# Scan's main loop written in a fixed order, with six groups' output products as seven block products in place of eight

## The chip, the cores and the metric

The kernel runs on one core of one Trainium2 chip. It is one launch for one layer of a network: a graph cross-attention, then a state-space scan, then a feed-forward part. The metric is the device time of the core in microseconds (us), lower is better. A core has a matrix engine (PE, whose weight loads are listed apart as PEld), a vector engine (DVE), a scalar engine (ACT), a general engine (POOL) and a queue that issues transfers (SP). Each engine runs its own instructions in the order in which they were put in its queue, and waits at an instruction until what that instruction needs is there. SBUF is the on-chip memory; PSUM is the small memory that PE writes its results to; the scan uses eight banks of it, each a tile of 128 partitions by 512 fp32 numbers.

## The reference, cut to what matters

Only the scan part (`_L0_attn_ref`) is touched. Its input is 16 sequences of 32 tokens, 512 tokens in all, 512 numbers each, all fp32. In outline:

```python
h = x * rsqrt(mean(x * x) + EPS) * norm_w
proj = einsum('bsd,od->bso', h, in_proj_w)         # gate 8192, hidden 8192, B and C 1024 each, dt 128
hBC = silu(causal_conv(hBC, conv_w, conv_b))       # 4 taps along the sequence
dt = softplus(dt + dt_bias);  A = -exp(A_log)      # 128 heads
L = exp(segsum(A * dt))                            # decay between two tokens of a sequence, per head
M = einsum('bcihn,bcjhn->bcijh', C, B) * L         # C and B are shared by the 16 heads of a group
y = einsum('bcijh,bcjhp->bcihp', M, hid * dt) + Dp * hid
yg = y * silu(gate)
ygr = yg * rsqrt(mean over the group's 1024 (yg * yg) + EPS)     # 8 groups
out = residual + einsum('bsd,od->bso', ygr * gnorm_w, out_proj_w)
```

The 8192 inner channels are 64 tiles of 128 channels; a group is 8 tiles (16 heads). So the scan is 8 groups of 8 tiles, and the output product sums over all 64 tiles.

## The kernel before, in words

The graph part comes first and takes the first 1300 us or so; the scan follows, and the feed-forward part ends the kernel. The scan first makes what all groups share: `hT` (the normed input, transposed: channels on partitions, tokens along the row), `dt` and `dA`, and `CB`, the products of C and B for each group (lines 1166 to 1247).

Then the main loop (lines 1347 to 1352) goes over the 8 groups. Its three stages:

- `inner(g)` makes the gate `gs` and the hidden values `hid` of a group. For each of its 8 tiles there are two projections (`project`, line 1181: four fp32 products of 128x128 weights with 512 tokens, accumulated in a PSUM bank of the pool `ps_p`, two banks). The gate gets a Silu on ACT (line 1260). The hidden tile gets its convolution (`convolve`): ACT writes the first tap out of PSUM (line 1188), DVE adds the three others, also out of PSUM (line 1193, three instructions), and ACT applies Silu (line 1196). With every tile from the second group on, one step of `parts` is taken: it loads small low-rank weights for the feed-forward part (nine small transfers for each piece) and splits a piece that came earlier into three bf16 parts, eight DVE instructions of 18 partitions (lines 167 to 173). There are ten pieces.
- `mix(g)` is the scan itself, tile by tile. PE transposes the hidden tile (`pht`, line 1289), DVE scales it by `dt` into `hd` (line 1291). For every second tile `decays` makes the decays of four heads: POOL multiplies `lei` by `dA` into `da` (line 1269), PE sums it (`pl`, line 1274), ACT takes the exponential `ed` (line 1279). DVE multiplies `ed` by `CB` into two tiles `el` (line 1302), PE makes the eight small products `py` (line 1310), DVE adds the skip term into `hid` (line 1314) and multiplies by the gate into `gs` (line 1315). ACT squares `gs`, POOL adds the squares into `ssq` (line 1321), ACT scales `gs` by `gnorm_w` (line 1322).
- `close(g)` makes the group's share of the output. PE sums `ssq` over the channels (`pn`, line 1329), DVE and ACT make the inverse root from it (line 1331 and the helper `rstd`, lines 70 to 80). The eight tiles `wo` of the output weights are loaded (line 1337). For each of the four blocks of 128 tokens, PE adds up eight products of 128x128 by 512 columns in a bank of `ps_o` (line 1342), and DVE adds the result, times the inverse root, into the residual `xt` (line 1345).

In the source `inner(g + 1)` stands ahead of `mix(g)` and `close(g)`, but the source does not set the order: a scheduler reorders the instructions of the whole kernel on every engine by its own priorities, within what data and buffers allow. Each tile comes from a pool, and a tag with `bufs` of n has n slots; a new tile waits until the one n before it on that tag has been read for the last time. The pools that count here: `ps_p`, `ps_m` (for `pht` and `pl`), `ps_y` (for `py` and `pn`) and `ps_o`, two PSUM banks each; six slots for the projection weights `win`; ten for `wo`; three for `hd` and `el`, two for `da`.

An fp32 product is two instructions on PE, so a profile counts two for each product in the source.

Of the kernel before, what the change touches and what calls it, by code (L numbers as in the profile page):

```python
# [8 lines left out]
F32 = mybir.dt.float32  # L9
# [3 lines left out]
AF = mybir.ActivationFunctionType  # L13
ALU = mybir.AluOpType
# [4 lines left out]
P = 128  # L19
B = 16  # L20
C = 32
D = 512
# [9 lines left out]
CB = 3  # L32
# [1083 lines left out]
def scan_part(nc, tc, cx, I, id32, ones, xt, u, rstd, lows):  # L1116
# [58 lines left out]
    def project(t, tag):  # L1175

        w = wpool.tile([P, 4, P], F32, tag="win", name=f"win{tag}", bufs=6)
        nc.sync.dma_start(out=w, in_=I["in_proj"][t])
        pp = ps_p.tile([P, D], F32, tag="p", name=f"pp{tag}")
        for k in range(4):  # L1180
            nc.tensor.matmul(pp, lhsT=w[:, k], rhs=hT[:, k], start=(k == 0), stop=(k == 3))  # L1181
        return pp

    def convolve(dst, t, tag):

        pp = project(NT + t, f"c{tag}")
        y = wk.tile([P, B, SEQ], F32, tag="cy", name=f"cy{tag}", bufs=3)
        nc.scalar.activation(  # L1188
            y.rearrange("p b s -> p (b s)"), pp, AF.Identity, bias=cb[:, t:t + 1], scale=cw[:, t, 3:4]
        )  # L1190
        pv = pp.rearrange("p (b s) -> p b s", b=B)
        for sh in (1, 2, 3):
            nc.vector.scalar_tensor_tensor(  # L1193
                y[:, :, sh:], pv[:, :, :SEQ - sh], cw[:, t, 3 - sh:4 - sh], y[:, :, sh:], ALU.mult, ALU.add
            )
        nc.scalar.activation(dst, y.rearrange("p b s -> p (b s)"), AF.Silu)


    wdt = wpool.tile([P, 4, P], F32, tag="win", name="wdt", bufs=6)
# [50 lines left out]
    parts = lows.load(low)  # L1250
    big = cx.enter_context(tc.tile_pool(name="sbig", bufs=2))

    def inner(g):

        gs = big.tile([P, TG, D], F32, tag="gs", name=f"gs{g}")
        hid = big.tile([P, TG, D], F32, tag="hid", name=f"hid{g}")
        for i in range(TG):
            t = g * TG + i
            pg = project(t, f"g{t}")
            nc.scalar.activation(gs[:, i], pg, AF.Silu)  # L1260
            convolve(hid[:, i], t, f"h{t}")
            if g > 0:
                next(parts, None)
        return gs, hid

    def decays(h):

        da = sm.tile([P, 4, 4, SEQ], F32, tag="da", name=f"da{h}", bufs=2)
        nc.gpsimd.tensor_tensor(  # L1269
            da, lei.unsqueeze(1).unsqueeze(1).to_broadcast([P, 4, 4, SEQ]),  # L1270
            dA[:, :, h:h + 4].rearrange("p q h -> p h q").unsqueeze(3).to_broadcast([P, 4, 4, SEQ]), ALU.mult,
        )
        pl = ps_m.tile([P, 4, 4, SEQ], F32, tag="m", name=f"pl{h}")
        nc.tensor.matmul(  # L1274
            pl.rearrange("p h q i -> p (h q i)"), lhsT=gt, rhs=da.rearrange("p h q i -> p (h q i)"),
            start=True, stop=True,
        )
        ed = sm.tile([P, 4, 4, SEQ], F32, tag="ed", name=f"ed{h}", bufs=2)
        nc.scalar.activation(ed, pl, AF.Exp)
        return ed  # L1280

    def mix(g, gs, hid):

        ssq = wk.tile([P, D], F32, tag="ssq", name=f"ssq{g}")
        for i in range(TG):
            t = g * TG + i
            pt = ps_m.tile([P, 4, P], F32, tag="m", name=f"pht{t}")
            for q in range(4):
                nc.tensor.transpose(pt[:, q], hid[:, i, q * P:(q + 1) * P], id32)
            hd = sm.tile([P, 4, 2, 64], F32, tag="hd", name=f"hd{t}")  # L1290
            nc.vector.tensor_tensor(
                hd, pt.rearrange("p q (h c) -> p q h c", h=2),
                dt[:, :, 2 * t:2 * t + 2].unsqueeze(3).to_broadcast([P, 4, 2, 64]), ALU.mult,
            )
            py = ps_y.tile([P, 4, P], F32, tag="y", name=f"py{t}")
            if i % 2 == 0:
                decay = decays(2 * t)
            els = []
            for j in range(2):

                el = sm.tile([P, 4, P], F32, tag="el", name=f"el{2 * t + j}")
                nc.vector.tensor_tensor(
                    el.rearrange("p q (b i) -> p q b i", b=4),
                    decay[:, 2 * (i % 2) + j].unsqueeze(2).to_broadcast([P, 4, 4, SEQ]),
                    CB[:, g].rearrange("p q (b i) -> p q b i", b=4), ALU.mult,
                )
                els.append(el)
            for q in range(4):
                for j in range(2):
                    nc.tensor.matmul(  # L1310
                        py[64 * j:64 * j + 64, q], lhsT=hd[:, q, j], rhs=els[j][:, q], start=True, stop=True
                    )
            pyf = py.rearrange("p q t -> p (q t)")
            nc.vector.scalar_tensor_tensor(hid[:, i], hid[:, i], dpc[:, t:t + 1], pyf, ALU.mult, ALU.add)
            nc.vector.tensor_tensor(gs[:, i], gs[:, i], hid[:, i], ALU.mult)
            if i == 0:
                nc.scalar.activation(ssq, gs[:, i], AF.Square)
            else:
                sq = wk.tile([P, D], F32, tag="sq", name=f"sq{t}")
                nc.scalar.activation(sq, gs[:, i], AF.Square)  # L1320
                nc.gpsimd.tensor_tensor(ssq, ssq, sq, ALU.add)
            nc.scalar.activation(gs[:, i], gs[:, i], AF.Copy, scale=gnw[:, t:t + 1])
        return ssq

    def close(g, gs, ssq):

        pn = ps_y.tile([P, 4], F32, tag="y", name=f"pn{g}")
        for q in range(4):
            nc.tensor.matmul(pn[:, q:q + 1], lhsT=ssq[:, q * P:(q + 1) * P], rhs=ones[:, 0:1], start=True, stop=True)
        mean = sm.tile([P, 4], F32, tag="gm", name=f"gm{g}")  # L1330
        nc.vector.tensor_scalar(mean, pn, 1.0 / (TG * P), None, ALU.mult)
        rs = sm.tile([P, 4], F32, tag="gr", name=f"gr{g}")
        rstd(sm, rs, mean, 4, f"gn{g}")
        wo = []
        for i in range(TG):
            w = wpool.tile([P, D], F32, tag="wo", name=f"wo{g}_{i}", bufs=TG + 2)
            nc.sync.dma_start(out=w, in_=I["out_proj"][g * TG + i])
            wo.append(w)
        for q in range(4):
            po = ps_o.tile([P, D], F32, tag="o", name=f"po{g}_{q}")  # L1340
            for i in range(TG):
                nc.tensor.matmul(  # L1342
                    po, lhsT=gs[:, i, q * P:(q + 1) * P], rhs=wo[i], start=(i == 0), stop=(i == TG - 1)
                )
            nc.vector.scalar_tensor_tensor(xt[:, q], po, rs[:, q:q + 1], xt[:, q], ALU.mult, ALU.add)  # L1345

    cur = inner(0)
    for g in range(G_M):
        nxt = inner(g + 1) if g + 1 < G_M else None
        ssq = mix(g, *cur)  # L1350
        close(g, cur[0], ssq)
        cur = nxt


def ffn_part(nc, tc, cx, I, id32, xt, layernorm, lows, out):
# [139 lines left out]
```

## Time and profile before

| what | value |
|---|---|
| time, median of 3 runs | 2353.34 us (2352.94 to 2354.5) |
| the profiled execution | 2354.35 us, of which the span is 2352.6 us |
| busy over the span | PE 92%, PEld 53%, DVE 72%, ACT 46%, POOL 35% |
| granted clock of PE, mean | 0.981 |
| main loop of the scan | from the first gate projection at 1402.08 to the last addition into `xt` at 2253.48 us |
| products of line 1342 | 512 instructions, 240.5 us busy |
| feed-forward part | from 2254.32 us to the end |

The profile is of one execution. A group of instructions is a line of the program with its engine, operation and tile names, then its count, its busy time and the mean of one in ns. In an answer in order of time, each row has its start and its length in us; a row of several instructions runs from the start of the first to the end of the last, and in brackets stands how long the engine was idle before it and what ended that. PE's instructions overlap, so two rows are best compared by their starts: from the start of one to the start of the next is what PE took for the work between.

### The profile page before, as it was taken

Reading aid. Unit: us, or ns where it says so; the run is one execution under the profiler, and the core shown is the slowest. Engines: PE = TensorE matmul, PEld = TensorE weight load, DVE = VectorE, ACT = ScalarE, POOL = GpSimd, SP = SyncE. Lnnn points to the kernel's source line nnn. Section 1 sums busy time; section 2 is a strip of 40 time slices with the busy share of each in tenths; the row PEclk is TensorE's granted clock in tenths of the full one; section 3 lists DMA queues with packets and bytes.
Section 4 is the critical chain, followed back from the end, with each engine's and each line's share of the span. In section 5 each row is a group of like instructions: output and inputs, shape, how many; then the busy total and the mean of one; then the engine's idle time right before and its main releaser. Section 6 shows DMA issues by size and latency. Waiting matters only on the chain. (4 is left out here: it accounts for less than half of the span.)

```text
span 2352.6 us, 88841 instructions
## 1 busy us (share of the span) xinstructions
PE 2168.6 (92%) x39234; PEld 1240.7 (53%) x39234; DVE 1696.2 (72%) x3674; ACT 1093.0 (46%) x2023; POOL 831.6 (35%) x897
## 2 busy tenths in 40 slices
PE   5598899999999988899999699999999999999979
PEld 2255555776557765577777344444444444444422
DVE  8488897998979999899999658455362635536543
ACT  6686677555765544455555123333242433333321
POOL 2155656555565555655655100011020202112200
PEclk9899999999999999999999799999999999999989
DMA  1324242232232322323111312211212121220000
GB/s 47 72 64 83 49 84 58 56 79 48 64 70 53 82 46 63 74 49 83 41 39 36 105 54 80 68 58 50 76 32 92 34 86 54 59 63 14 28 37 18
DMA packets 121625, 137.99 MB, mean 59 GB/s; under 512 B 18398, under 2 KB 79506, under 8 KB 121154
## 3 DMA queue, kind: packets, MB, share of 16 engines
q1 hardware_dynamic: 121240, 132.32, 22.6%
q8 instruction: 308, 5.05, 0.9%
q14 instruction: 77, 0.63, 0.1%
HBM read 77.02 MB, written 12.85 MB: 38 GB/s over the span
## 5 line engine op out<-in xcount | busy, mean ns | idle before, releaser
L890 POOL TENSOR_TENSOR EN<-e,rz 128x480 f32<-128x480 f32 x344 | 342.3, 995 | 496.7 <-DVE rz L888 405.0
L915 PE MATMUL u<-WA,DD 128*32 128x128 bf16 (+1 forms) x16512 | 411.8, 247 | 18.3 <-issue 17.7
L920 ACT COPY us<-u 128x512 f32<-128x512 f32 x516 | 301.6, 586 | 153.0 <-PE u L915 136.0
L915 PEld LDWEIGHTS <-DD 128*32 128x32 f16 x16512 | 337.2, 97 | 51.8 <-issue 50.4
L811 POOL TENSOR_TENSOR DD<-fs,crep 128x480 f16<-128x480 f32 (+2 forms) x344 | 349.6, 1017 | 0.0
L875 ACT ACTIVATE e<-s,smc 128x480 f32<-128x480 f32 x344 | 227.3, 661 | 252.3 <-PE s L870 220.4
L943 PEld LDWEIGHTS h<-e,us 128*32 128x32 f32 (+1 forms) x11008 | 245.9, 125 | 134.2 <-issue 68.4
L943 PE MATMUL h<-e,us 128*32 128x30 f32 (+1 forms) x11008 | 278.8, 210 | 32.6 <-issue 15.6
L1193 DVE SCALAR_TENSOR_TENSOR cyh<-ppch,t_conv_w,cyh 128x496 f32<-128x496 f32 (+2 forms) x192 | 137.5, 716 | 221.7 <-ACT cyh L1188 217.7
L862 DVE TENSOR_REDUCE c<-s 128x16 bf16<-128x480 f32 x344 | 220.8, 642 | 81.2 <-PE s L853 77.9
L1269 POOL TENSOR_TENSOR da<-lei,dA 128x512 f32<-128x512 f32 x32 | 40.5, 1266 | 612.6 <-PE pl L1274 577.2
L1342 PE MATMUL po<-wo,gs 128*128 128x512 f32 x512 | 240.5, 605 | 10.5 <-DVE xt L1345 10.3
L1181 PE MATMUL ppch<-hT,winch 128*128 128x512 f32 x512 | 232.2, 593 | 0.0
L1181 PE MATMUL ppg<-hT,wing 128*128 128x512 f32 x512 | 231.9, 593 | 0.0
L896 DVE STREAM_TRANSPOSE e<-EN 128x512 f32<-128x512 f32 x344 | 225.2, 655 | 0.0
L882 DVE TENSOR_REDUCE z<-e 128x16 f32<-128x480 f32 x344 | 220.0, 640 | 0.4 <-ACT e L875 0.4
L541 ACT ACTIVATE sgn<-kd 128x512 bf16<-128x512 f32 x256 | 153.1, 598 | 53.0 <-PE kd L540 50.1
L751 DVE TENSOR_SCALAR oh<-it,rank 128x512 bf16<-128x512 f16 x512 | 156.9, 369 | 11.9 <-PE pp L705 11.9
L853 PEld LDWEIGHTS <-DD 128*32 128x32 f16 x5504 | 80.7, 96 | 158.1 <-issue 132.4
L853 PE MATMUL s<-DX,DD 128*32 128x120 f16 x5504 | 141.5, 221 | 19.0 <-DMA DX<-DD 15.3
L1181 PEld LDWEIGHTS ppch<-hT,winch 128*128 128x128 f32 x512 | 93.7, 190 | 122.7 <-issue 122.3
L1181 PEld LDWEIGHTS ppg<-hT,wing 128*128 128x128 f32 x512 | 95.8, 190 | 114.0 <-issue 114.0
(327 smaller groups left out, 2846.0 us busy)
## 6 DMA issues: line engine op xcount, KB each, us to landing
DX<-DD SPq DMA_DIRECT2D x456, 90.0 KB
wo<-in_out_proj SPq DMA_DIRECT2D x64, 256.0 KB
wing<-in_in_proj SPq DMA_DIRECT2D x64, 256.0 KB
winch<-in_in_proj SPq DMA_DIRECT2D x64, 256.0 KB
crep<-dC SPq DMA_DIRECT2D x128, 64.0 KB
dS<-so SPq DMA_DIRECT2D x32, 256.0 KB
fs<-dS SPq DMA_DIRECT2D x128, 64.0 KB
wincB<-in_in_proj SPq DMA_DIRECT2D x8, 256.0 KB
```

The costliest lines, as they stand in the source:

```text
L811: nc.gpsimd.tensor_tensor(d[:, :, m0 - n0:n1 - n0], win, crep[:, :, m0:n1].unsqueeze(3).to_broadcast([P, 4, n1 - m0, K]), ALU.subtract,)
L853: nc.tensor.matmul(s[rh, j * 4 * QB:(j + 1) * 4 * QB].rearrange("p (b q) -> p b q", b=4), lhsT=d[:, h, c0:c0 + 32], rhs=dx[:, h, :, c0:c0 ...
L862: nc.vector.tensor_reduce(c, live["s", at, gi].rearrange("p (i q) -> p i q", q=QB), AX.X, ALU.max, negate=True)
L875: nc.scalar.activation(e, s.rearrange("p (i q) -> p i q", q=QB), AF.Exp, scale=smc)
L882: nc.vector.tensor_reduce(z, e, AX.X, ALU.add)
L890: nc.gpsimd.tensor_tensor(en[:, :, :QB], e, rz.unsqueeze(2).to_broadcast([P, NI, QB]), ALU.mult)
L896: nc.vector.transpose(e.rearrange("p i q -> p (i q)"), en.rearrange("p i q -> p (i q)"))
L915: nc.tensor.matmul(u[rh, jj], lhsT=d[:, h, c0:c0 + 32], rhs=WA[k][:, h].rearrange("p b o -> p (b o)"), start=(jj == 0 and k == 0), stop=(k ...
L920: nc.scalar.copy(us[:, j - jj:j + 1], u)
L943: nc.tensor.matmul(h[r:r + co, pr, q0:q0 + QB], lhsT=us[:, j, b * co:(b + 1) * co], rhs=e[:, 4 * j + b, :QB], start=npair > 1, stop=True, ...
L1181: nc.tensor.matmul(pp, lhsT=w[:, k], rhs=hT[:, k], start=(k == 0), stop=(k == 3))
L1342: nc.tensor.matmul(po, lhsT=gs[:, i, q * P:(q + 1) * P], rhs=wo[i], start=(i == 0), stop=(i == TG - 1))
```

## The change

The main loop gets an order written out by hand, and the output products of six of the eight groups are computed in another form. What it does:

- From the start of the main loop to the end of the scan, `tc.manual_schedule()` makes every engine and the transfer queue take their instructions in the order of the source.
- The source order is now by step. Step `i` of group `g` is: the gate projection of tile `i` of the next group (`gate`); the rest of the convolution of the step before (`convolve_steps` is now a generator that stops after ACT's first tap), and with it the step of `parts`; `gated(i - 1)`: skip term, gate, squares and scaling of the tile before; `turn(i)`: transposes, in odd steps the decays of the next two tiles (`ahead`: `pl` and `ed`), in even ones POOL's `da` for those decays (`spread`), then `hd`, the two `el`, and the load of one `wo`; the convolution's projection and its first tap; `summed(i)`; `outputs(i)`: the products `py`. So POOL makes `da` one step before PE reads it.
- For groups 0 to 5, two tiles and two token blocks at a time, the 2x2 block product of `gs` with `wo` is made by seven block products in place of eight (the form of Strassen and Winograd). `operands` makes the sums that this needs: per pair of tiles four DVE instructions on halves of `wo` (128x256) and four on token halves of `gs` (128x256). `summed` calls the first four in an even step and the other four in the step after; the last pair's come after the last step.
- `close_by_seven` then makes, for each half `h` of the tokens, 4 pairs x 7 products of 128x128 by 256 columns, accumulated over the pairs in seven half banks: for `h` = 0 in the banks of `ps_p` and `ps_m`, for `h` = 1 in those of `ps_o` and `ps_y`. The inverse root (`root`) is made between the two halves. One ACT copy, seven DVE additions and four DVE multiply-adds of 128x256 then bring the seven sums into `xt`.
- Group 6 keeps the old form, spread over the steps of group 7, half a token block a step; group 7's closing follows at the end.
- Slots: `wo` 8 in place of 10, `hd` and `el` 2 in place of 3, `da` 1 in place of 2.

```diff
+    cx.enter_context(tc.manual_schedule())
...
+    def summed(self, i):
+            if self.g + 2 >= G_M:
+                return
+            if self.sums is None and i % 2 == 0 and i:
+                self.sums = operands(self.g, i // 2 - 1, self.gs, self.wo)
+            if self.sums:
+                got = next(self.sums)
...
+    def operands(g, p, gs, wo):
...
+        nc.vector.tensor_tensor(t1, b12, b11, ALU.subtract)
+        nc.vector.tensor_tensor(t2, b22, t1, ALU.subtract)
+        nc.vector.tensor_tensor(b12, b22, b12, ALU.subtract)
+        nc.vector.tensor_tensor(t4, b21, t2, ALU.subtract)
+        yield
+        nc.vector.tensor_tensor(s1, a21, a22, ALU.add)
+        nc.vector.tensor_tensor(s2, s1, a11, ALU.subtract)
+        nc.vector.tensor_tensor(a21, a11, a21, ALU.subtract)
+        nc.vector.tensor_tensor(s4, a12, s2, ALU.subtract)
+        yield [(a11, b11), (a12, b21), (s4, b22), (a22, t4), (s1, t1), (s2, t2), (a21, b12)]
...
+    def close_by_seven(g, gs, ssq, wo, pairs):
+        for h in range(2):
+            banks = [
+                pool.tile([P, 2, HN], F32, tag=tag, name=f"po{g}_{h}_{tag}{k}")
+                for pool, tag in (((ps_p, "p"), (ps_m, "m")), ((ps_o, "o"), (ps_y, "y")))[h]
+                for k in range(2)
+            ]
+            acc = [banks[k // 2][:, k % 2] for k in range(7)]
+            for p, products in enumerate(pairs):
+                for k, (x, y) in enumerate(products):
+                    nc.tensor.matmul(
+                        acc[k], lhsT=x[:, h], rhs=y, start=(p == 0 and k % 2 == 0), stop=(p == TG // 2 - 1),
...
+            if h == 0:
+                rs = root(g, ssq)
...
-    cur = inner(0)
+    for i in range(TG):
+        gate(0, i)
+        end_of(current(0, i))
+    spread(0)
+    ahead(0)
+    last = None
     for g in range(G_M):
-        nxt = inner(g + 1) if g + 1 < G_M else None
-        ssq = mix(g, *cur)
-        close(g, cur[0], ssq)
-        cur = nxt
+        mix = Mix(g)
+        conv = None
+        for i in range(TG):
+            if g + 1 < G_M:
+                gate(g + 1, i)
+            end_of(conv)
+            conv = None
+            if i:
+                mix.gated(i - 1)
+            mix.turn(i)
+            if g + 1 < G_M:
+                conv = current(g + 1, i)
+                next(conv)
+            else:
+                next(last, None)
+            mix.summed(i)
+            mix.outputs(i)
+        end_of(conv)
+        mix.gated(TG - 1)
+        for _ in range(2):
+            mix.summed(TG)
+        end_of(last)
+        last = mix.closing()
+        if g + 2 != G_M:
+            end_of(last)
+            last = None
```

## The prediction

> **What bounds the kernel now.** The page shows PE busy for 92% of the span. The last slices are the scan (from slice 22) and the feed-forward part (the last two). The chain that ended last covers 3% of the span only, so I went on by stretches: one period of the scan's loop (from a row of `py` to the row that answers to it a group later), its tail, and the loop as a whole.
>
> ```profile
> PE 2168.6 (92%) x39234; PEld 1240.7 (53%) x39234; DVE 1696.2 (72%) x3674; ACT 1093.0 (46%) x2023; POOL 831.6 (35%) x897
> PE   5598899999999988899999699999999999999979
> DVE  8488897998979999899999658455362635536543
> PEclk9899999999999999999999799999999999999989
> ...
> 1515.41:1619.69 104.28, 102.73 (x364) 48.18 (x363) 50.63 (x74) 36.34 (x52) 15.70 (x11) 1.00 0.21 61
> 2143.00:2254.30 111.30, 99.97 (x479) 49.47 (x477) 68.79 (x103) 37.55 (x53) 27.61 (x20) 1.00 0.05 15
> 1402.08:2254.30 852.22, 832.77 (x2953) 388.11 (x2951) 435.91 (x678) 287.74 (x414) 119.22 (x92) 1.00 0.19 55
> ```
>
> In a stretch the columns are its length, then the busy time of PE, PEld, DVE, ACT and POOL, the clock and the transfers. PE is busy for 102.7 of a period's 104.3 us at full clock and DVE for half. So the loop is PE's work, and what changes that work, or makes PE wait, changes the time. PE's prices come from its rows in order of time, DVE's from its own:
>
> ```profile
> 1398.61 1.05 PE L1246 MATMUL pcb<-Cg,Bg 128*128 128x128 f32 x8
> 1399.50 2.74 PE L1181 MATMUL ppcC<-hT,wincC 128*128 128x512 f32 x6
> 1402.08 3.60 PE L1181 MATMUL ppg<-hT,wing 128*128 128x512 f32 x8
> 1405.52 1.09 PE L1181 MATMUL ppch<-hT,winch 128*128 128x512 f32 x2
> ...
> 1619.69 1.09 PE L1310 MATMUL py<-el,hd 128*64 128x128 f32 x16
> 1620.71 1.09 PE L1289 MATMUL pht<-id,hid 128*128 128x128 f32 x8
> 1621.64 3.60 PE L1181 MATMUL ppg<-hT,wing 128*128 128x512 f32 x8
> ...
> 1475.13 2.22 DVE L1193 SCALAR_TENSOR_TENSOR cyh<-ppch,t_conv_w,cyh 128x496 f32<-128x496 f32 x3 [2.58 <-ACT cyh L1188]
> 1539.07 0.68 DVE L1302 TENSOR_TENSOR el<-ed,CB 128x512 f32<-128x512 f32 x1
> 1540.33 1.10 DVE L1302 TENSOR_TENSOR el<-ed,CB 128x512 f32<-128x512 f32 x1
> L169 DVE TENSOR_TENSOR lw<-lw,lpb 18x344 f32<-18x344 f32 x6 | 3.0, 500 | 0.1
> L169 DVE TENSOR_TENSOR lw<-lw,lpb 18x168 f32<-18x168 f32 x2 | 0.6, 322 | 0.1
> 1309.71 2.89 POOL L179 MEMSET lb<- 128x1376 bf16 x3
> 1311.90 2.38 DVE L95 TENSOR_SCALAR n<-h,lnmv_f,lnr_f 128x512 f32<-128x512 f32 x1
> ```
>
> Start to start, a projection of 8 instructions takes 1405.52 - 1402.08 = 3.43 us, so 0.429 us for 512 columns. Eight instructions of 128 columns (`pcb`) take 0.89 us, 0.111 each: in proportion, though each loads new 128x128 weights. `py` takes 1.02, `pht` 0.93, `pl` (two of 512) 0.86, `pn` 0.92.
>
> **The products.** A group's output was 64 instructions of 512 columns, 27.47 us. It becomes 2 halves x 28 products x 2 = 112 of 256 columns. No row has 256 fp32 columns with new weights each time; it lies between the rows of 128 and 512, both proportional, so 0.2146 us and 24.04 us (bounds 0.215 and, from `pcb`, 0.222, 24.9). Gain 3.43 us a group, 20.6 in six.
>
> **PE's whole list in the new order**, if it never waits. Ahead of the loop: 8 x 2 projections, one `pcb`, one `pl`, 56.7 us. A step of groups 0 to 6 is gate 3.43, `pht` 0.93, in odd steps `pl` 0.86, convolution 3.43, `py` 1.02: 8.81 even, 9.67 odd, 74.0 for eight; 518.0 for seven groups. Six closings of 24.04 + 0.92: 149.8. Group 7: steps of `pht`, half an old block (3.43), `py`, three with `pl`: 45.6, and `pn` 0.9. Its closing 27.47 + 0.92, and after it the last addition 0.95: 29.3. Sum 800.3 against 852.2. The rest is what PE waits for.
>
> **DVE's extra work.** The two rows of `lw` give a line: 0.41 us for 256 numbers, 0.67 of them in 344. Four `operands` instructions, mostly each on the one before: 1.6 us in each of six steps, and twice at the end of a group. Eleven of the final sums are some 5 us per half, in place of two 0.75 us additions. Does it stay beside PE? Take an even step from its gate projection at 0. The convolution's three instructions (2.2; the row of x3) can begin at 0, as ACT's first tap ended then; gating 0.74 + 0.03 + 0.69 ends at 3.7. `hd` must wait for `pht`, done at 4.36 + 0.2; then `hd` 0.67 and two `el`. These were 0.60 apart alone and up to 1.05 when POOL worked (0.68 against 1.10 in the rows). They end at 6.5 to 7.3, and `py` needs them at 7.79: 0.5 to 1.3 us to spare. `operands` ends at 8.1 to 9.5; the next convolution may start at 8.8, and it has 0.8 us of room before its `hd`. Odd steps have 0.86 more. So I cost this at nothing; the cover is PE's step, and without it DVE's 9.6 us (all two-operand rows at the slow value) against PE's mean 9.24 would cost 0.36 x 36 steps = 13 us.
>
> The Trainium skill speaks against this change here: "SBUF — State Buffer", section "SBUF: two separate sides", says that POOL and a DVE instruction with two SBUF inputs take a shared port in turn, and whoever is second waits for the other's whole instruction. By it, with 1.5 POOL instructions of about 1.4 us a step, DVE would lose up to 2.1 us a step and need some 9.4 us, about 5 us more in all. The rows show 0.42 lost at an `el`, which is what the sum uses.
>
> **Waits that I expect.**
> - The bank of the seven products. The first half's third product needs the second bank of `ps_p`, which the last convolution still reads until 2.2 us after the last `py`; PE gets there after two products, 0.86. In order, nothing goes ahead: 1.4 us, six times, 8.4. (Bounds 0 to 2.5, if DVE is a us late.)
> - The low-rank splits. Eight DVE instructions, 3.2 us a piece from their rows, now stand ahead of `gated` and `hd` in the queue. Seven fall in group 0, six of them in steps with `operands`: DVE then needs 2.2 + 3.2 + 1.5 + 0.7 + 1.6 + 1.8 = 11.0 against 9.24, so 1.7 x 6 = 10; the three in group 1 some 3. Sum 13 (bounds 6, as if half were room, and 10 x 3.2 = 32). Before they lay beside projections.
> - `root` of group 6 inside group 7: DVE stands 2.9 us for ACT's two table loads (the row of `gm` to the row of `gr`, 1551.71 to 1554.62), then the addition; the next `py` is some 2.2 late. In the other groups it lies beside the second half's 12 us.
> - The final sums. First half: `pn` ends at about 14.4 us after the last `py`, the root 17.6, eleven sums 22.5; the next gate wants the bank at 26.4. Second half: done some 5 us into the next step, `hd` there at 4.6. Nothing, with 4 us of cover; past that, its banks stop PE.
> - Hand-overs in a fixed order. Before, PE lost 104.28 less its list of 101.9, 2.4 us a group, of which 1.3 were `po` waiting for `xt`. I take 0.1 us for each of 64 steps, 6.4 (bounds 0 and 0.5 x 64 = 32).
>
> **Queues.** SP now has `wo` between the projection weights, and one waits for the closing's second half to free slots; six `win` slots hold three steps, 27 us, of cover. In group 0 the nine small loads wait for a split and stand ahead of the next weights: these are issued some 10 us into a step and landed 2 us later, wanted 4 us into the next one, so 2 us of cover. `wo` for group 7 come free only in its steps 6 and 7, 4 us or more ahead of need. POOL's `da` moves a step earlier, so its 1.3 us leave PE's path; the slots of `hd`, `el` and `da` are read out a step before they are wanted. ACT's exponentials now each bring two 1.28 us table loads, in a step where ACT has 4 to 5 us of work in 9.7.
>
> **Ahead of the loop.** POOL's memsets move from 1309.7 into the loop. `n` took 2.38 us beside them, 0.55 on another execution of that line: 1.2 us gained after the reordered `hT` (bounds 0 and 1.8). The feed-forward part has the same order after the end of the scan; nothing.
>
> **Sum.** 800.3 + 8.4 + 13 + 2.2 + 6.4 = 830.3 for the loop, against 852.2: 21.9, and 1.2 ahead: 23.1 us faster. The profiled execution took 2354.35, its span 2352.6 and 1.75 around it; the median of the runs is 1.0 below it. So 2353.3 - 23.1 = 2330.
>
> **Rivals.**
> - DVE is slower in the steps than worked out and takes part of PE's gain: 13 us as above and more on the splits, 2340 to 2348. For it: every step's queue has PE and DVE waiting on each other once. Against it: half a us or more of room at `py`.
> - The fixed order makes it slower: PE waits at `py` in each of the 56 steps, since `hd` stands behind the convolution, the splits and the gating of the step before. It decides from 23.1 / 56 = 0.41 us a step, that is when DVE needs 9.7 us a step; at 10.3 us it would lose 1.06 x 56 = 59, less 23: 2390. Against: even the slow rows give 9.6.
> - The products don't gain, as weights aren't hidden: load (0.19 us) and 0.215 in turn would be 45.4 us a closing, 108 us more in six: 2438. Against: `pcb` at 0.111 with new weights each time.
> - The waits are smaller (splits find room, hand-overs none): 800.3 + 8 + 6 + 2, 37 us faster, 2316.
>
> **Chances.** My case, 2323 to 2340: 0.58. Smaller waits, 2310 to 2323: 0.13. DVE takes part, 2340 to 2348: 0.11. Within 0.2% (4.7 us, about what a measurement can tell from none): 0.07. Slower: 0.11, nearly all by DVE's queue. So faster 0.82. The range is 2314 to 2353: it leaves out the slow cases and the edge of the fast.
>
> **What would show it.** Right: 384 instructions of 512 columns fewer and 672 of 256 more, the latter 0.215 us apart; a period near 101 us in groups 2 to 5; a gap of about 1.4 us after the second of the seven products, ended by DVE's convolution; steps of 10.5 to 11 us in group 0 with PE waiting for `el` ahead of `py`; nothing there later. Wrong: PE waiting for `el` in most steps, gate projections waiting for the final sums or for weights, or 256 columns at 0.3 us and more.

## The result, and the profile after

The changed kernel takes 2318.7 us (median of 4 runs, 2312.2 to 2324.9) against 2353.1 (median of 4, 2350.1 to 2354.5) for the kernel before: a ratio of 0.9855, 95% interval 0.9826 to 0.9884. It is 34.4 us faster, where 23.1 were forecast; 2330 was predicted, and the time lies within the range of 2314 to 2353. The direction was right and so was most of the mechanism, but the sum came this close by luck: two larger errors in it have opposite signs. The changes of order that came with the products gain far more than the products, and the fixed order, taken by itself, is a loss. The experiments show both.

The page of the changed kernel, its line of busy times and two lines of its slices:

```profile
PE 2131.8 (92%) x39522; PEld 1300.3 (56%) x39522; DVE 1835.5 (79%) x3974; ACT 1140.4 (49%) x2073; POOL 840.7 (36%) x897
PE   5599899999999998899999789989999999999979
DVE  8488897999989999889999763788786967866643
```

PE has 288 instructions more than before, 384 of 512 columns fewer and 672 of 256 columns more, and is busy for 36.8 us less; DVE is busy for 139 us more, since it makes the operands and the final sums. Slice 27 (1506 to 1564 us, the end of group 0) falls to 8 on PE, where before had 9 in all slices of the loop, and DVE stands at 8 in slices 27 and 28 and higher than before from slice 26 to slice 36.

Stretches of the changed kernel (length, busy time of PE, PEld, DVE, ACT and POOL with their instructions, clock, share of transfers, GB/s): the loop, a period of a middle group, and a part of group 0.

```profile
1400.65:2227.74 827.09, 793.18 (x3241) 444.68 (x3240) 582.53 (x1002) 341.12 (x475) 133.53 (x99) 0.99 0.20 62
1659.19:1757.28 98.09, 96.95 (x418) 57.21 (x417) 74.12 (x124) 42.73 (x59) 16.52 (x11) 1.00 0.20 65
1460.00:1560.00 100.00, 88.66 (x363) 48.73 (x362) 86.21 (x156) 44.09 (x59) 20.70 (x20) 0.98 0.14 44
```

From here on "the loop" runs from the first gate projection to the first transposition of the feed-forward part, which both kernels have: before 1402.08 to 2263.49, 861.4 us (the prediction's 852.2 and 9.2 us of the way into the feed-forward part); after 827.1 us. The loop is 34.3 us shorter, so it holds the whole gain. It is also the cleaner measure, because the graph part ahead of it moved by several us between kernels that have the same instructions there (the loop began at 1385.6 to 1401.0 us in the runs below). Where the loop's time lies is read from the starts of `pn`, one in each group:

| kernel | first `pn` after the loop's start | from `pn` to `pn` | rest | loop |
|---|---|---|---|---|
| before | 148.5 | 103.7, 105.1, 105.1, 105.1, 105.1, 105.1, 54.8 | 29.0 | 861.4 |
| after | 156.9 | 104.4, 98.1, 98.1, 98.1, 98.1, 96.4, 45.4 | 31.7 | 827.1 |

(The first `pn` comes after a different amount of output products in the two, so the first two columns are to be read together.) A middle group gains 7 us. Groups 0 and 1 lose time that the middle groups don't. PE in the closing of group 1, then in a step of group 1, in order of time:

```profile
1647.29 1.09 PE L1352 MATMUL py<-el,hd 128*64 128x128 f32 x16
1648.32 1.13 PE L1438 MATMUL po_p<-wo,gs 128*128 128x256 f32 x4
1650.58 0.67 PE L1438 MATMUL po_p<-wo,osum 128*128 128x256 f32 x2 [1.13 <-DVE cyh L1194]
1651.09 0.59 PE L1438 MATMUL po_p<-wsum,gs 128*128 128x256 f32 x2
1651.52 1.03 PE L1438 MATMUL po_m<-wsum,osum 128*128 128x256 f32 x4
1652.38 0.59 PE L1438 MATMUL po_m<-wo,gs 128*128 128x256 f32 x2
...
1592.38 3.60 PE L1181 MATMUL ppch<-hT,winch 128*128 128x512 f32 x8
1597.55 0.43 PE L1352 MATMUL py<-el,hd 128*64 128x128 f32 x2 [1.57 <-DVE el L1333]
1599.21 1.97 PE L1352 MATMUL py<-el,hd 128*64 128x128 f32 x14 [1.24 <-DVE el L1333]
1601.11 5.69 PE L1181 MATMUL ppg<-hT,wing 128*128 128x512 f32 x8
1606.64 0.60 PE L1318 MATMUL pht<-id,hid 128*128 128x128 f32 x4
```

Four instructions of 256 columns, two products, take 1652.38 - 1651.52 = 0.86 us, 0.216 each, as predicted. The third product starts 2.26 us after the first, where 0.86 of work lies between: the predicted gap of 1.40 us, ended by the convolution. In the step below it PE stands twice at `py` for `el`. The last row shows something that the prediction did not use: `pht` is four instructions a tile, not eight.

### The profile page after: what moved, and what is told of

Read it like the earlier page. It is cut to its first block, busy times and chain, and to the rows that moved or that the text cites. A ratio compares the mean times of both kernels' runs of the same rounds, so it can differ in the third digit from the quotient of the medians.

```text
span 2316.7 us, 89754 instructions
## 1 busy us (share of the span) xinstructions
PE 2131.8 (92%) x39522; PEld 1300.3 (56%) x39522; DVE 1835.5 (79%) x3974; ACT 1140.4 (49%) x2073; POOL 840.7 (36%) x897
## 5 line engine op out<-in xcount | busy, mean ns | idle before, releaser
L915 PE MATMUL u<-WA,DD 128*32 128x128 bf16 (+1 forms) x16512 | 414.1, 248 | 16.6 <-issue 16.4
L1368 POOL TENSOR_TENSOR ssq<-ssq,sq 128x512 f32<-128x512 f32 x56 | 89.9, 1606 | 592.6 <-ACT sq L1367 592.6
L1181 PE MATMUL ppg<-hT,wing 128*128 128x512 f32 x512 | 238.3, 609 | 0.0
L870 PE MATMUL s<-c,idb 128*128 128x480 bf16 x344 | 130.4, 379 | 5.6 <-DVE c L862 2.7
```

Source lines behind the costliest of these rows:

```text
L915: nc.tensor.matmul(u[rh, jj], lhsT=d[:, h, c0:c0 + 32], rhs=WA[k][:, h].rearrange("p b o -> p (b o)"), start=(jj == 0 and k == 0), stop=(k ...
```

## The experiments

Each kernel was timed beside the kernel before on the same chip; ratios are to that. There the kernel before took 2341.9 to 2349.6 us, so times in us compare only roughly between the runs.

**Order and products apart.** The change has two parts, and three kernels fill in the other corners.

The fixed order alone, with eight products in all groups:

```diff
         def summed(self, i):
-            if self.g + 2 >= G_M:
-                return
+            return
...
-            return (close_by_seven if self.g + 2 < G_M else close)(self.g, self.gs, self.ssq, self.wo, self.pairs)
+            return close(self.g, self.gs, self.ssq, self.wo, self.pairs)
```

> The changed kernel's fixed order, but all eight groups close in the old form: no sums of operands on DVE, 64 instructions of 512 columns a group. Theory (most of the gain is the order, the products add their 3.43 us a group less the 1.40 us that PE waits for the second bank): each of six closings takes 28.3 us in place of the 26.5 measured, 10.8 us more in all; the waits of groups 0 and 1 shrink by some 8 us, since DVE has no sums to make there. So some 2321 us, between 2314 and 2329, and a period of 99.9 us in groups 2 to 5. Rival (the gain is the products, and the order only spares DVE's share of it): 2340 us or more, and a period of 102 us or more.

Measured: 2328.7 us, ratio 0.9903 (0.9881 to 0.9925), loop 832.5, period 100.0. The period is as expected and the time lies at the slow end of the theory's range: groups 0 and 1 lose 17.7 us over middle groups, where the changed kernel loses 21.3, so their waits shrank by 3.6 us and not by 8.

The new source and the seven products, but with the scheduler placing the instructions:

```diff
-    cx.enter_context(tc.manual_schedule())
```

> The changed kernel's source with the seven products, but the scheduler sets the order of the instructions in the main loop as before. Theory (the order is most of the gain): the products' 20.6 us at most are left, and the scheduler's small pieces on PE keep costing what they cost before, 5.8 us a group over the instructions' own time: 2330 to 2350 us. Rival (the products are the gain): 2322 us or less.

Measured: 2281.4 us, ratio 0.9701 (0.9674 to 0.9727), loop 793.8. Both my theory and its reason fell: without the fixed order the kernel is not slower than the changed one but 33.3 us faster in the loop.

The same without the seven products, so the new source in the scheduler's hands (both edits above):

> The changed kernel's source order, steps and operands ahead, but without the fixed order (the scheduler places the instructions) and with all eight groups closed by the old products. Nothing is left out. It splits what the run with the scheduler and seven products gained over before (loop 793.8 against 861.4) into products and order. My theory: the products are worth 3.4 less 0.1 to 0.4 us a group, 18 to 20 us in six, and the rest is the order in which the steps are written: loop 812 to 814, period of a group 100.0 us, total 2298 to 2303. Rival (the fixed order had hidden the worth of the products, which take DVE's and PE's waits with them): loop 825 to 840, total 2313 to 2328. Rival (the products are worth little, as with the fixed order, where they brought 5.4 us): loop 797 to 802.

Measured: 2304.8 us, ratio 0.9836 (0.9815 to 0.9856), loop 810.9, period 100.0. The mark needs care here. In the two kernels with the new source and eight products, the first transposition of the feed-forward part starts 6.6 us after the last addition into `xt`; in all other kernels it starts 9.2 to 9.6 us after it. So their loops read some 2.6 us too short against the others: 813.5 here on equal terms, as my theory expected, with the time 1.8 us above its range. The table therefore ends the loop at the last addition into `xt`, as the prediction does.

| to the last addition, us | eight products | seven products | products bring |
|---|---|---|---|
| scheduler's order, new source | 804.28 | 784.53 | 19.75 |
| fixed order, new source | 825.84 | 817.87 | 7.97 |
| the fixed order costs | 21.56 | 33.34 | |

Against 852.15 before, the new source by itself brings 47.87 us (its step order, POOL's operands a step ahead, the other numbers of slots, and group 6's closing laid beside group 7, which were not taken apart), the seven products 19.75, and the fixed order takes 33.34 back: 34.28 us less in all. By the starts of `pn`, of what the new source brings, 5.1 us lie in each middle group and 12.2 in the period of group 7 (54.8 to 42.6). A period of the scheduler's kernels, first with eight products, then with seven, each in its own stretch:

```profile
1534.70:1634.70 100.00, 100.00 (x369) 48.17 (x368) 51.83 (x74) 42.51 (x58) 15.20 (x11) 1.00 0.22 64
```

```profile
1494.53:1591.20 96.67, 96.67 (x417) 57.30 (x416) 68.46 (x124) 43.29 (x59) 15.26 (x11) 1.00 0.22 66
```

PE is busy for the whole of both. The products are worth 3.3 us in each of six groups where PE is the limit, with DVE's extra 16.6 us a group beside it at no cost. What the fixed order takes had to be found next; by the marks it lies in groups 0 and 1, at the second bank, and in group 7.

**The second bank.** The first half's banks are taken in the other order, so that the bank which the convolution still reads is wanted four products later:

```diff
-                for pool, tag in (((ps_p, "p"), (ps_m, "m")), ((ps_o, "o"), (ps_y, "y")))[h]
+                for pool, tag in (((ps_m, "m"), (ps_p, "p")), ((ps_o, "o"), (ps_y, "y")))[h]
```

> The changed kernel with the two banks of ps_m taken ahead of those of ps_p for the first half of the seven products, so that the bank that the last convolution still reads is wanted by the seventh product in place of the third. Theory (the gap of 1.13 us in the profile, 1.40 from the second product's end, is that bank alone): no gap, a period of 96.7 us in place of 98.09 in groups 2 to 5, and 8 us less in six groups, 2308 to 2313 us. Rival (another operand is late at the same place, so the wait only moves to the next product): the period stays at 98 us.

Measured: 2308.0 us, ratio 0.9814 (0.9785 to 0.9844), loop 820.3, period 96.7: 6.8 us shorter. PE in the closing of group 1, fixed order, banks swapped:

```profile
1641.74 1.09 PE L1352 MATMUL py<-el,hd 128*64 128x128 f32 x16
1642.76 1.13 PE L1438 MATMUL po_m<-wo,gs 128*128 128x256 f32 x4
1643.73 0.59 PE L1438 MATMUL po_m<-wo,osum 128*128 128x256 f32 x2
1644.16 0.59 PE L1438 MATMUL po_m<-wsum,gs 128*128 128x256 f32 x2
1644.59 1.03 PE L1438 MATMUL po_p<-wsum,osum 128*128 128x256 f32 x4
```

The gap is gone, and in groups 1 to 5 nothing takes its place. In group 0 another wait does, for the operands of the last pair, which DVE makes late there:

```profile
1546.91 1.03 PE L1438 MATMUL po_m<-wo,gs 128*128 128x256 f32 x4
1549.66 0.70 PE L1438 MATMUL po_m<-wo,osum 128*128 128x256 f32 x2 [1.72 <-DVE osum L1422]
```

So the first `pn` stays at 156.9 us, and the 6.8 us are five groups' 1.4. The period is now that of the scheduler's order, so in groups 2 to 5 the fixed order costs nothing else.

**The splits.** In the changed kernel the low-rank splits begin with group 1's tiles, made during group 0. Beginning them in the prologue (group 0's own projections, ahead of the scan), where DVE has room:

```diff
         yield from convolve_steps(made[g][1][:, i], t, f"h{t}")
-        if g > 0:
-            next(parts, None)
+        next(parts, None)
```

> The changed kernel with the steps of the low-rank loads and splits begun with the first group's projections, so that seven of the ten splits lie beside the 55 us of projections ahead of the scan and three in the first steps of group 0. Theory (the 14.1 us that group 0 and the 6.5 us that group 1 take over a quiet group are DVE's splits standing ahead of the gating, and the clock that PE loses behind such a wait): group 1 as fast as groups 2 to 5, group 0 at most 6 us slower, 14 to 18 us faster than the changed kernel, 2301 to 2305 us. Rival (the first groups are slow because weights come late behind the small loads, or because POOL and DVE hold each other up there): groups 0 and 1 lose what they lost, 2314 us or more.

Measured: 2323.0 us, ratio 0.9877 (0.9851 to 0.9903), loop 835.3, 8.2 longer than in the changed kernel; not the gain expected. Group 1 is clean (98.1 at once), but the prologue is not. The waits of PE in this kernel's loop (what waited, for what, us in total, times, longest), and one of them in order of time:

```profile
PE ppg L1181 <- DMA wing<-in_in_proj: 15.7, 4, 4.4
...
1423.79 3.60 PE L1181 MATMUL ppch<-hT,winch 128*128 128x512 f32 x8
1431.72 5.37 PE L1181 MATMUL ppg<-hT,wing 128*128 128x512 f32 x8 [4.34 <-DMA wing<-in_in_proj]
```

Projections wait for weights. SP's queue shows why: the nine small loads of a piece (2.6 us of issuing) wait for the slot that a split frees, and the next weights stand behind them, issued at 1428.81 when PE wanted them at about 1427.4. The loss moved from DVE's queue to SP's.

So a second try put the small loads on ACT's queue, and took the swapped banks as well:

```diff
-                    nc.sync.dma_start(out=w[2 * k:2 * k + 2], in_=self.I[f"b{n}T"][:, cols])
+                    nc.scalar.dma_start(out=w[2 * k:2 * k + 2], in_=self.I[f"b{n}T"][:, cols])
```

> The changed kernel with its fixed order, and three edits together: the low-rank splits begin in the prologue, their small loads are issued by ACT's queue in place of SP's, and the two banks of the seven products are swapped. Nothing is left out. My theory (the fixed order costs time at three places that it cannot step round: the splits ahead of DVE's gating, SP's queue behind the small loads, the second bank; nothing else): group 0's and group 1's waits fall from 20.6 us to 2 to 5, those of the projection gates for weights are gone, the period is 96.7 from group 1 on, loop 800 to 806, total 2286 to 2296; what is left against the scheduler's 793.8 is the root of group 6 in group 7. Rival (the fixed order costs in every step, by hand-overs): loop 815 or more, as the periods of groups 2 to 5 already equal the scheduler's this rival can lie only in groups 0, 1, 6 and 7.

Measured: 2296.8 us, ratio 0.9814 (0.9779 to 0.9849), loop 816.2, first `pn` at 156.1, then 96.7 five times, 96.4 and 48.4. Half of the theory held: the waits for weights are gone, and group 1 is clean. But the prologue and group 0 together are no shorter, so 800 to 806 was missed. The rival's 815 was met, but not for its reason, as groups 1 to 5 run at the scheduler's period. ACT issues the nine loads in 4.2 us, and `ed` and the gates stand behind them. ACT in this kernel, group 0's first step:

```profile
1453.87 4.20 ACTq L185 DMA_DIRECT2D lw<-in_b3T  x9
1458.10 1.28 ACT L1292 ACT_TABLE_LOAD   x1 [3.68 <-DMA lw<-in_b3T]
1459.39 0.60 ACT L1292 ACTIVATE ed<-pl 128x512 f32<-128x512 f32 x1
1460.02 1.29 DVE L1332 TENSOR_TENSOR el<-ed,CB 128x512 f32<-128x512 f32 x2 [2.61 <-ACT ed L1292]
1460.77 0.43 PE L1351 MATMUL py<-el,hd 128*64 128x128 f32 x2 [2.38 <-DVE el L1332]
```

The first repair thus moved the cost to SP's queue, and the second most of it to ACT's: with the banks alike it gained 4.1 us (820.3 to 816.2). To price the cause itself, it was taken away: with the banks swapped, first the splits and their loads left out, then POOL's addition, then both.

```diff
-                w = pool.tile([LR, width], F32, tag="lw", name=f"lw{n}_{c}")[:, :cols.stop - c]
-                for k in range(9):
-                    nc.sync.dma_start(out=w[2 * k:2 * k + 2], in_=self.I[f"b{n}T"][:, cols])
                 yield
-                self.split(pool, t[:LR, cols], w, self.of[1], f"b{n}_{c}")
```

> The fixed order with the two banks swapped (loop 820.3 us, first pn 156.9 us into it, next period 103.0, then 96.7), and the low-rank splits with their small loads left out: the weights of the low-rank part stay zero, so the result of that part is left out too; the scan itself is whole. Theory A (the splits, standing ahead of gating in DVE's queue, are the whole of what groups 0 and 1 lose against the scheduler's order, where the first pn came 141.0 us in): first pn 141 to 143, next period 96.7, loop 798 to 802. Theory B (the splits are only the smaller half; the rest is DVE's el standing behind POOL's instructions, which in a fixed order meet in every even step): first pn 147 to 152, loop 806 to 815. Under both the last two periods stay at 96.4 and 45.4, since no split lies there.

Measured: loop 797.6 (2285.5 us, ratio 0.9750, 0.9720 to 0.9780), first `pn` at 140.5, then 96.7. Theory A, with the loop 0.4 us below its range: the splits are all that groups 0 and 1 lose, 22.7 us of loop (14.3 in the steps of group 0, 6.3 in those of group 1, 2.0 in the closing of group 0, at the wait shown above).

```diff
-                nc.gpsimd.tensor_tensor(ssq, ssq, sq, ALU.add)
```

> The fixed order with the two banks swapped (loop 820.3 us, first pn 156.9 us into it, then 103.0, 96.7 and at the end 45.4), and POOL's addition to ssq left out, seven a group: the norm of each group's rows then counts only its first tile. Nothing else of POOL's is taken away. It prices what DVE loses to POOL. Theory A (splits): of the 20.6 us lost in groups 0 and 1 the pair of el beside POOL, 2.35 us in place of 1.28, accounts for 1.07 us in about nine of sixteen steps: first pn 149 to 153, next period 99 to 102, loop 806 to 814 with 2 to 4 us more in group 7. Theory B (POOL is the whole loss): first pn 141 to 143, period 96.7 at once, loop 796 to 800. Theory C (no price, as the pair of el stays as long without it): loop 819 to 821.

Measured: loop 808.3 (2291.4 us, ratio 0.9774, 0.9741 to 0.9807), first `pn` at 150.3, next period 100.8, last 42.9. Theory A again.

> Both of these left out together: the splits with their loads, and POOL's addition to ssq; banks swapped, fixed order. The low-rank part works on zero weights, and the norms count one tile of eight. It gives the floor of the fixed order with DVE at ease. Expected: first pn 141 to 142, periods of 96.7 and then 95 to 96.4 and 41.5 to 43.5, loop 792 to 797, at or just above the scheduler's 793.8. If the fixed order itself costs in every step or at its closings, the loop stays above 800.

Measured: loop 794.4 (2275.1 us, ratio 0.9708, 0.9677 to 0.9739), first `pn` at 140.5, then 96.7, at the end 95.7 and 42.9. That is the scheduler's 793.8 within 0.6 us.

With these the account of the fixed order closes: 794.4 with DVE at ease; 3.2 more for POOL's addition (797.6), all of it in groups 6 and 7; 22.7 more for the splits (820.3), of which 13.9 are there without POOL's addition too (808.3 - 794.4); 6.8 more for the bank (827.1). How splits and POOL add up is seen on DVE in group 0. Changed kernel, one step on DVE, from convolution to convolution:

```profile
1486.97 2.21 DVE L1194 SCALAR_TENSOR_TENSOR cyh<-ppch,t_conv_w,cyh 128x496 f32<-128x496 f32 x3
1489.10 0.32 DVE L167 CAST lpb<-lw 18x344 bf16<-18x344 f32 x1
...
1491.74 0.56 DVE L173 SCALAR_TENSOR_TENSOR lb<-lpb,lof,lb 18x344 bf16<-18x344 bf16 x1
1492.23 0.73 DVE L1361 SCALAR_TENSOR_TENSOR hid<-hid,t_Dp,py 128x512 f32<-128x512 f32 x1
1492.99 0.69 DVE L1362 TENSOR_TENSOR gs<-gs,hid 128x512 f32<-128x512 f32 x1
1493.60 0.68 DVE L1324 TENSOR_TENSOR hd<-pht,dt 128x512 f32<-128x512 f32 x1
1494.20 2.35 DVE L1333 TENSOR_TENSOR el<-ed,CB 128x512 f32<-128x512 f32 x2
1496.48 0.41 DVE L1419 TENSOR_TENSOR osum<-gs 128x256 f32<-128x256 f32 x1
...
1497.94 2.22 DVE L1194 SCALAR_TENSOR_TENSOR cyh<-ppch,t_conv_w,cyh 128x496 f32<-128x496 f32 x3
```

DVE does not stop: 10.97 us a step, where PE's work is 8.96. So PE waits at `py`, behind 3.1 us of splits and an `el` pair of 2.35 us. Without POOL's addition the same pair, in the run for that, takes 1.28:

```profile
1480.80 1.28 DVE L1333 TENSOR_TENSOR el<-ed,CB 128x512 f32<-128x512 f32 x2
1482.01 0.42 DVE L1413 TENSOR_TENSOR wsum<-wo 128x256 f32<-128x256 f32 x1
```

The scheduler's kernel makes the same splits. It does them from 1406 to 1467 us, mostly in the prologue, in the pauses between convolutions, with the loads placed where they hold up no weights.

**POOL's operand a step ahead.** `da` in the step that needs it:

```diff
             if i % 2:
+                if 2 * t + 2 < H_M:
+                    spread(2 * t + 2)
                 ahead(2 * t + 2)
-            elif 2 * t + 4 < H_M:
-                spread(2 * t + 4)
```

> The changed kernel, but POOL's operand da for the next pair of steps is issued in the odd step that uses it, just before pl, in place of a step earlier. Nothing is left out. My theory (the step ahead keeps POOL off PE's path in a fixed order): da now stands behind the step's addition to ssq in POOL's queue; in the odd step of the trace of after that ends with py at 1709.56 that addition runs from 1706.71 to 1708.46, so da would end at about 1709.7 and pl starts then, not at 1705.17. PE stands 4.6 us in each odd step, 28 of them in groups 0 to 6: 129 us, plus 1 to 2 us each where the clock is reduced after the wait. Loop 930 to 1010 us against 827, total 2420 to 2500. Rival (POOL is idle three quarters of the time, so only da's own 1.25 us comes onto the path, and in groups 0 and 1 it falls into waits that are there already): at most 31 x 1.25, 39 us: loop 845 to 866, total 2335 to 2358.

Measured: 2462.2 us, ratio 1.0500 (1.0470 to 1.0531), loop 974.5, 147 us longer than after; middle periods 116.1. The theory held, with three such waits a group in place of four (the group's first odd step follows a tile whose squares go straight to `ssq`, without POOL's addition). POOL in such a step, and PE in the same:

```profile
1736.21 1.68 POOL L1368 TENSOR_TENSOR ssq<-ssq,sq 128x512 f32<-128x512 f32 x1 [6.85 <-ACT sq L1367]
1737.85 1.25 POOL L1278 TENSOR_TENSOR da<-lei,dA 128x512 f32<-128x512 f32 x1
```

```profile
1734.23 0.60 PE L1318 MATMUL pht<-id,hid 128*128 128x128 f32 x4
1739.15 2.08 PE L1288 MATMUL pl<-da,gt 128*128 128x512 f32 x2 [4.32 <-POOL da L1278]
1741.02 4.29 PE L1181 MATMUL ppch<-hT,winch 128*128 128x512 f32 x8
```

A wait of 4.32 us costs about 6 (18.0 a period for three), since `pl` then takes twice its 1.02 us and the projection 4.29 in place of 3.60.

**A further step.** Without the fixed order, group 6 in seven products too, beside group 7:

```diff
-            if self.g + 2 >= G_M:
+            if self.g + 1 >= G_M:
...
-            return (close_by_seven if self.g + 2 < G_M else close)(self.g, self.gs, self.ssq, self.wo, self.pairs)
+            return (close_by_seven if self.g + 1 < G_M else close)(self.g, self.gs, self.ssq, self.wo, self.pairs)
...
-                for pool, tag in (((ps_p, "p"), (ps_m, "m")), ((ps_o, "o"), (ps_y, "y")))[h]
+                for pool, tag in (((ps_p, "p"), (ps_m, "m") if g + 2 < G_M else (ps_o, "o")), ((ps_o, "o"), (ps_y, "y") if g + 2 < G_M else (ps_p, "p")))[h]
```

> The changed kernel without the fixed order, and group 6 closed by seven products too, its first half on the banks of ps_p and ps_o, its second on ps_o and ps_p, beside the steps of group 7. Nothing is left out. A version that may beat the others. If PE bounds group 7, the gain is 16 more instructions of 256 columns fewer, 3.4 us: loop 790 to 791 against 793.8. If group 7 is bound by DVE (16 el and hd of 0.7 us, gating, and now 12 us of operands and 10 of final sums in 45 us), or the second half waits for the first half's sums to free its banks, the loop is 794 or longer, up to 800.

Measured: 2285.8 us, ratio 0.9753 (0.9729 to 0.9776), loop 802.8: 9.0 longer than with six groups, outside both expectations, though the second had named the wait for the first half's sums. Two waits, 2.73 us for a final sum that frees a bank and 3.71 us at the last `pn` for POOL's `ssq`, with slower instructions behind them (the 64 of the last closing take 30.4 us in place of 27.5), take more than 16 instructions give. The best kernel of the study is the changed one without the fixed order, at 2281.4 us (ratio 0.9701).

## Why the prediction was right or wrong

The working forecast 830.3 us for the loop, 839.5 to the mark used here; it measured 827.1.

- **PE bounds the loop, and 256 columns take 0.2146 us:** right. PE is busy for 793 of 827 us; the pitch (start to start) is 0.216, and the counts of 384 and 672 came as said. The products' gain of 3.43 us a group is 3.3 where PE never waits. But the prediction drew 20.6 of its 21.9 us from the products. In the fixed order the new source with eight products already brings 26.3 (852.15 to 825.84) and the products 8.0; of the 11.8 that they fall short of their 19.75, 6.8 is the bank, and 5.0, by subtraction, the operands in DVE's queue in groups 0 and 1.
- **`pht` at 0.93 us a step:** this step failed. The quoted row of `pht` with x8 is two tiles that the scheduler had put side by side; a tile is four instructions, 0.44 us, and the group's count (256 for 64 tiles) would have shown it. It makes PE's list 64 x 0.49 = 31 us too long. The steps measure 8.53 and 9.39 us, not 8.81 and 9.67. The same slip made the kernel before look tight: the parts of its group add up to 102.3 us (the prediction has 101.9), and to 98.4 with the right `pht`, so a group of 104.28 lost 5.9 us and not 2.4. That is room which the new source uses. Mostly for the same reason the middle period came at 98.1 us and not near 101.
- **The second bank, 8.4 us:** right in place and cause, and in size where it bounds. The gap is 1.40 us in group 1, and the swapped banks give back 6.8 in all, since in group 0 the late operands stand behind it.
- **The low-rank splits, 13 us:** right in place and cause, too small: 22.7. DVE's step of 11.0 us was right (10.97), but it was set against 9.24 us of PE's work, which is 8.96; group 0's steps average 10.74 and lose 14.3 us instead of 10, group 1's lose 6.3 instead of 3, and the closing of group 0, which had no such term, loses 2.0.
- **POOL and DVE:** the row used, 0.42 us lost at an `el`, was too small; the kernel before has an `el` of 1.75 us too, 1.07 over 0.68. A pair loses 1.07 us, and taking the addition away is worth 12.0 us (820.3 to 808.3). The section "SBUF: two separate sides" of the Trainium skill's "SBUF — State Buffer", which was weighed and not used, states that the second of the two waits for the other's whole instruction; the pair of 2.35 us beside POOL and 1.28 without agrees with it. But it is a price only where DVE is late: in the scheduler's kernel the 128 `el` take 128.8 us in place of 96.0, and that kernel is 33 us faster in the loop. The fixed order shows it too: without splits and without the addition, the `el` meet `da` in the middle groups instead (106.7 us in all, against 88.6 with the addition), and that loop is 3.2 us shorter.
- **Hand-overs 6.4 us and the root of group 6, 2.2:** too small together. The list without the slip is 769.1 us, 778.3 to the mark; the floor of 794.4 leaves 16.1, and POOL's addition 3.2 more, so 19.3 in place of 8.6. Steady steps show 0.21 us each, not 0.1; group 7's eight steps with `pn` take 50.3 us for 42.6 of work, with the root's wait in its third (1.42 and 1.18 us) and an `el` pair of 2.35 in six of them.
- **The sum:** -31.2 for `pht`, -1.6 for the bank, +9.7 for the splits, +10.7 for hand-overs and group 7: 839.5 becomes 827.1. The last term is what is left over, not a measurement of its own.
- **The operands and final sums at no cost:** right from group 2 on. In groups 0 and 1 DVE has no cover, and the operands' work there is part of what the splits cost.
- **POOL's `da` a step ahead:** called a gain off the path; in a fixed order it is what 147 us hang on. **Ahead of the loop, 1.2 us:** the loop began 1.4 us earlier, but kernels with the same instructions there differ by 15, so this stays open.
- **The rivals:** weight loads not hidden, and DVE making the kernel slower, did not come. (The first was also summed wrongly: 45.4 us a closing against the new 24.04 is 128 us more in six, so 2458 and not 2438.) "Smaller waits" gave 2316 and was nearest in time, but not in cause: the waits were larger. None of the cases compared the fixed order with a scheduler working on the same new source, and there it loses 33 us.

## What to carry to other kernels

Price an operation by its count over the whole kernel divided by the number of tiles, because a row in order of time can join two. When a source order and a fixed schedule come in one change, run the new source without the fixing. In a fixed order, occasional work (here ten splits with small loads) must be placed by hand on every queue it uses, where that queue has room: two attempts to move it moved most of the wait, from DVE to SP and from SP to ACT.

## What the runs showed of the hardware

PE's granted clock can fall after short pauses. After waits of 1.57 and 1.24 us with a burst of 0.43 us between them, eight projection instructions that take 3.60 us took 5.69; the stretch around it, in the changed kernel:

```profile
1597.00:1607.00 10.00, 8.22 (x28) 4.49 (x29) 9.76 (x19) 1.53 (x3) 3.06 (x2) 0.66 0.09 28
```

The clock is 0.66 there and 1.00 in the middle groups. The length alone does not decide it: after the root of group 6 the waits of 1.42 and 1.18 us left the rest of `py` at 1.09 us and the clock at 1.00 in the changed kernel, while the same pair in the kernel with its loads on ACT's queue was followed by 1.97 at a clock of 0.88 (over 10 us each), and its last period is 48.4 us in place of 45.4. In group 0 of the changed kernel itself, waits of 0.71 and 1.24 us before 1507.58 were followed by a projection of 3.70 us, and waits of 0.73 and 1.24 before 1519.44 by one of 4.79. The Trainium skill's "TensorE: Matmul & The Clock Gate", Part 1, states half the clock after an idle window of about 3.4 us, and that this window runs freely. The waits of 4.3 us above agree with the length, but here 2.8 us idle within 3.2 was enough; that the window runs freely no run here shows.

An issue of nine small transfers takes 2.6 us on SP's queue and 4.2 us on ACT's, and on ACT it stands in the way of its work.
